# A graph-attention layer on one core: the tail of its first part re-ordered, W loaded in eight pieces

## The chip, the cores and the metric

The kernel runs on one core of a Trainium2 chip. A core has five engines with a queue of their own each: TensorE (PE in the profile, its weight loads PEld), VectorE (DVE), ScalarE (ACT), GpSimd (POOL) and SyncE (SP, which here only issues DMAs). An engine executes its queue in order; between engines there are semaphores. The metric is the device time of the whole kernel in microseconds; lower is better.

## The reference

There are N = 3327 nodes with D = 1024 features. adj is an N x N int32 matrix of zeros and ones with some 17 ones in a row. All else is float32.

```python
h = jnp.maximum(_layernorm(x, axis=-1), 0.0)
f = h @ Wf + bf
g = h @ Wg + bg
e = jax.nn.relu(f @ g.T)
scores = jnp.where(adj > 0, e, NEG)
attention = jax.nn.softmax(scores, axis=1)
out = x + attention @ (h @ W + bW)
```

## The kernel before

Only the neighbours of a node count, so the kernel (`edge_path`) turns each row of adj into a list of neighbours, and then gathers the rows of h that a list names. It has two parts, and each engine's order of work is written out by hand in both.

**Part 1** goes through the rows in NT = 26 tiles of 128 nodes (the last has 127) in stages i = 0 to 22. For each tile:

- `load_adj` brings 128 x 3327 integers into one of five buffers (`kpool`, tiles named r). It is issued by SP five stages ahead, when the buffer's former tile has been searched.
- `degrees` (ScalarE, L691) turns the integers to floats and counts them; `keys` (GpSimd, L698) multiplies the row by 1 to N, in two halves.
- `segments` (VectorE, L761) takes the eight largest keys out of each of 16 stretches of a row; `listed` (VectorE, L768 to L776) makes a list of 24 out of these 128 and writes it to pay. `store_lists` and `store_left` (SP) write the lists to pd and the candidates to cd, both in DRAM.
- layernorm: `load_x` (SP, six buffers in `ln`, tiles named xt); `measured` and `rooted` compute mean and deviation, on VectorE for odd tiles (L707, L709) and in two passes on ScalarE for even ones (L721 to L725); `inverted` (VectorE, L729) takes the reciprocal; `scaled` (ScalarE, L735) writes h in place; `store_h` (SP, L739) stores it to hd in DRAM.

The tables `at_load`, `at_stats` and `at_scale` say in which stage a tile's x is loaded, measured and scaled. Beside this, TensorE multiplies Wf by the transposed Wg in stages 4 to 21 (`product`, L831; the result is A_sb, and WgT is the tile that W_sb takes over).

**The order of the nodes.** Nodes are sorted by degree. `one_hot` (L784) makes a row of 48 bins from a degree; `before` and `after` (TensorE, L792 and L795) count with it into pre; `placed` (L800) takes a node's place among those of its own degree. The tail of part 1 (from L965) does this for the last tiles, then sums over bins (L1015 to L1022), makes rank, lo and hi (L1024 to L1028), compares them with a counting row (ohp at L1034, ohs and place at L1040 to L1046), and 26 small multiplications (L1049) invert the order into perm (L1057). In the tail stand also the searches of tiles 23, 24 (`late`) and 25 (`last`) and the layernorm of the last tiles.

**Part 2** takes 26 tiles of 128 nodes in the order of perm. For each tile it gathers lists from pd (ps), candidates from cd for nodes of high degree (cts), and rows of hd (G) with indirect DMAs that GpSimd issues (L635), one per list place. q = h A + b is TensorE's (L1209); scores are dot products on VectorE (L1222); ScalarE takes the exponential and weighs rows; TensorE sums and transposes them (L1260) and multiplies by W (L1287). The order comes from a planner (`planned`), and is the same before and after the change. The first two tiles' q are made ahead (L1069 to L1092) from two gathers of hd, which stand first in GpSimd's queue after perm; then, in the kernel before, comes the load of W as one DMA of 4 MB (L1064), then the first list gather. bWb, the broadcast bias of W, is loaded by SP (L1124).

SP's DMAs share eight semaphores in turn: each issue waits until the DMA eight before it has landed, and SP's queue is in order.

Of the kernel before, what the change touches and what calls it, by code (L numbers as in the profile page):

```python
# [575 lines left out]
def edge_path(ctx: ExitStack, tc: tile.TileContext, x, adj, Wf, bf, Wg, bg, W, bW, out, flag):  # L576
# [67 lines left out]
    with ExitStack() as part1:  # L644
# [33 lines left out]
        def load_x(t):  # L678
            xt = xs[t] = ln.tile([P, D], FP, name="xt")
            for b, m in pieces(t):  # L680
                nc.sync.dma_start(xt[b : b + m], x[t * P + b : t * P + b + m, :])
# [168 lines left out]
        at_load = {t: t + 2 for t in range(18)} | {18: 20, 19: 21, 20: 21, 21: 22, 22: 22, 23: 22, 24: 22}  # L850
        at_stats = {t: t + 4 for t in range(16)} | {16: 20, 17: 20, 18: 21, 19: 22, 20: 22}
        at_scale = {t: t + 5 for t in range(16)} | {16: 21, 17: 21, 18: 22}
        of = lambda table, i: [t for t in range(NT) if table.get(t) == i]

        with tc.manual_schedule(engines={
# [59 lines left out]
            for i in range(NT - 3):  # L915
                degrees(i + 2)
                keys(i + 2, nc.gpsimd)
                if i < 3:
                    for c in (2 * i + 2, 2 * i + 3):
                        transposed(WgT[:, :, c * P : (c + 1) * P], A_sb[:, c, :D])  # L920
                        empty()
# [15 lines left out]
                if i + 5 < NT:  # L937
                    load_adj(i + 5)
                for c in range(KD):
# [23 lines left out]
                for t in of(at_load, i):  # L963
                    load_x(t) if t >= NT - 3 else None
            late, last = NT - 2, NT - 1  # L965
            degrees(last)
            keys(last, nc.gpsimd)
            empty()
            one_hot(late, last)
            one_hot(last, NT)  # L970
            for t in (NT - 7, NT - 6):
                inverted(t)
                scaled(t)
            store_left(NT - 4)
            store_h(NT - 7)
            load_x(last)
            store_h(NT - 6)
            measured(NT - 5, True)
            rooted(NT - 5)
            measured(NT - 4, False)  # L980
            rooted(NT - 4)

            s = 0
            after(counted - 1)
            for t in range(counted, NT):
                before(t)
                segments(NT - 3, s, s + 2)
                s += 2
                placed(t)
                after(t)  # L990
                if t == NT - 3:
                    for u in (NT - 5, NT - 4):
                        inverted(u)
                    for u in (NT - 5, NT - 4):
                        scaled(u)
                        store_h(u)
            segments(NT - 3, s, s + 1)
            measured(NT - 3, True)
            rooted(NT - 3)
            measured(late, False)  # L1000
            rooted(late)

# [15 lines left out]
            inverted(NT - 3)  # L1018
            scaled(NT - 3)
            store_h(NT - 3)  # L1020
# [3 lines left out]
            nc.vector.tensor_add(ranki, rank, rp)  # L1024
            lo = c1.tile([P, NT], I32, name="lo")
            nc.vector.tensor_scalar(lo, ranki, P - 1, None, op0=ALU.bitwise_and)
            hi = c1.tile([P, NT], I32, name="hi")
            nc.vector.tensor_scalar(hi, ranki, 7, None, op0=ALU.logical_shift_right)  # L1028
            inverted(late)
            scaled(late)  # L1030
            store_h(late)
            measured(last, True)
            rooted(last)
            nc.vector.tensor_tensor(  # L1034
                ohp, lo[:, :, None].to_broadcast([P, NT, P]), iotap[:, None, :].to_broadcast([P, NT, P]), op=ALU.is_equal
            )
            inverted(last)
            scaled(last)
            store_h(last)
# [5 lines left out]
            )  # L1045
            nc.vector.tensor_scalar(place[:, :, 1, :], ohs, part, None, op0=ALU.mult)  # L1046
            ps = p_mm.tile([P, CB], FP, name="ps_A")
            for t in range(NT):
                nc.tensor.matmul(  # L1049
                    ps[:, : 2 * NT], ohp[:, t, :], place[:, t, :, :].rearrange("p a s -> p (a s)"),  # L1050
# [321 lines left out]
```

## Time and profile before

| | |
|---|---|
| median of 3 runs | 1243.84 us (1241.71 to 1244.11) |
| the profiled execution | 1279.55 us, span 1277.8 us, mean TensorE clock 0.951 |
| PE, DVE, ACT, POOL busy | 88%, 89%, 48%, 69% of the span |
| DMA | 374.46 MB, mean 293 GB/s |
| adj, x loads, h stores: median from issue to landing | 13.2, 13.5, 10.5 us |

The profile is of one execution, and its times count from the span's start. Part 1 lies from 0 to some 230 us; part 2 follows and overlaps with its end. A row of a timeline gives start and length, engine, line, operation, output and input, and in brackets how long the engine was idle before it and what ended this. A DMA's row is that of its issue; its data land later. The granted clock concerns TensorE alone.

### The profile page before, as it was taken

Reading aid. Unit: us, or ns where it says so; the run is one execution under the profiler, and the core shown is the slowest. Engines: PE = TensorE matmul, PEld = TensorE weight load, DVE = VectorE, ACT = ScalarE, POOL = GpSimd, SP = SyncE. Lnnn points to the kernel's source line nnn. Section 1 sums busy time; section 2 is a strip of 40 time slices with the busy share of each in tenths; the row PEclk is TensorE's granted clock in tenths of the full one; section 3 lists DMA queues with packets and bytes.
Section 4 is the critical chain, followed back from the end, with each engine's and each line's share of the span. In section 5 each row is a group of like instructions: output and inputs, shape, how many; then the busy total and the mean of one; then the engine's idle time right before and its main releaser. Section 6 shows DMA issues by size and latency. Waiting matters only on the chain. (4 is left out here: it accounts for less than half of the span.)

```text
span 1277.8 us, 14478 instructions
## 1 busy us (share of the span) xinstructions
PE 1127.0 (88%) x4632; PEld 720.7 (56%) x4632; DVE 1134.0 (89%) x2167; ACT 618.1 (48%) x941; POOL 876.2 (69%) x677
## 2 busy tenths in 40 slices
PE   2799980887987899997999799999999999999995
PEld 2566650555646467655766465665655665555553
DVE  6999977778798999999999979898999999999991
ACT  5899978234418256544644254453323433333250
POOL 8999975277576667677677657557676776766711
PEclk9899985798998999999999899999999999989998
DMA  9999996689768989989899879679987998989941
GB/s 369 418 379 397 404 347 233 209 313 340 268 204 298 340 274 328 313 311 311 284 325 293 305 221 332 216 259 330 311 299 236 339 270 305 271 291 296 321 110 52
DMA packets 101803, 374.46 MB, mean 293 GB/s; under 512 B 14747, under 2 KB 18490, under 8 KB 98519
## 3 DMA queue, kind: packets, MB, share of 16 engines
q0 software_dynamic: 80624, 290.96, 67.9%
q1 hardware_dynamic: 21094, 82.49, 17.1%
q8 instruction: 38, 0.62, 0.2%
q14 instruction: 47, 0.39, 0.1%
HBM read 344.11 MB, written 29.30 MB: 292 GB/s over the span
## 5 line engine op out<-in xcount | busy, mean ns | idle before, releaser
L635 POOL DMA_INDIRECT G<-hd,ps x454 | 524.3, 1155 | 243.6 <-issue 103.1
L1222 DVE CUSTOM_DVE_ANT_0 junk<-G,q 128x1024 bf16<-128x1024 f32 x468 | 601.6, 1286 | 40.0 <-DMA G<-hd,ps 28.7
L1209 PE MATMUL p_q<-A_sb,hT 128*128 128x342 f32 x1152 | 361.1, 463 | 14.7 <-ACT hT L1205 5.2
L1287 PE MATMUL p_o<-W_sb,yT 128*128 128x512 f32 x832 | 368.2, 598 | 3.7 <-ACT yT L1283 3.3
L1272 DVE SCALAR_TENSOR_TENSOR G<-G,sc 128x1024 f32<-128x1024 f32 x257 | 330.9, 1287 | 11.5 <-ACT G L1245 10.4
L1209 PEld LDWEIGHTS p_q<-A_sb,hT 128*128 128x128 f32 x1152 | 217.5, 195 | 124.0 <-issue 17.4
L1287 PEld LDWEIGHTS p_o<-W_sb,yT 128*128 128x128 f32 x832 | 158.2, 192 | 194.3 <-issue 184.7
L1260 PE MATMUL p_y<-ident,G 128*128 128x128 f32 x1688 | 208.2, 276 | 21.4 <-issue 11.5
L1260 PEld LDWEIGHTS p_y<-ident,G 128*128 128x128 f32 x1688 | 192.5, 143 | 53.5 <-issue 25.5
L1256 ACT ACTIVATE G<-G,sc 128x1024 f32<-128x1024 f32 x185 | 197.2, 1137 | 0.1
L698 POOL TENSOR_TENSOR r<-r,iotaj 128x1664 f32<-128x1664 f32 (+3 forms) x50 | 183.8, 3762 | 15.0 <-ACT r L691 15.0
L1298 ACT ACTIVATE xp<-p_o,rs 128x512 f32<-128x512 f32 x50 | 33.1, 682 | 213.1 <-DMA out_dram<-xp,perm 80.9
L831 PE MATMUL ps_A<-WgT,WfT 128*128 128x342 f32 x432 | 132.2, 465 | 2.4 <-ACT WfT L826 2.4
L761 DVE MAX8 cand<-r 128x8 f32<-128x208 f32 (+2 forms) x416 | 119.1, 360 | 4.0 <-POOL r L698 3.7
L831 PEld LDWEIGHTS ps_A<-WgT,WfT 128*128 128x128 f32 x432 | 82.5, 195 | 43.5 <-issue 3.3
L1215 ACT COPY q<-p_q 128x342 f32<-128x342 f32 x72 | 31.8, 445 | 128.0 <-PE p_q L1209 51.5
L691 ACT ACTIVATE r<-r 128x3327 f32<-128x3327 int32 (+3 forms) x27 | 77.3, 2862 | 8.1 <-DMA r<-in_adj_dram 8.1
L1283 ACT COPY yT<-p_y 128x512 f32<-128x512 f32 x52 | 29.9, 585 | 75.6 <-remote 43.9
L1205 ACT COPY hT<-p_t 128x512 f32<-128x512 f32 x48 | 27.4, 587 | 67.7 <-PE p_q L1209 32.4
L635 POOL DMA_INDIRECT xp<-in_x_dram,perm x25 | 41.5, 1660 | 22.1 <-ACT xp L1298 15.0
L1202 PE MATMUL p_t<-ident,G 128*128 128x128 f32 x192 | 31.7, 289 | 24.6 <-ACT hT L1205 9.1
L1305 POOL DMA_INDIRECT out_dram<-xp,perm x25 | 31.0, 1239 | 30.3 <-DMA xp<-in_x_dram,perm 22.9
(139 smaller groups left out, 687.2 us busy)
## 6 DMA issues: line engine op xcount, KB each, us to landing
r<-in_adj_dram SPq DMA_DIRECT2D x24, 1663.5 KB, 13.2
xt<-in_x_dram SPq DMA_DIRECT2D x25, 512.0 KB, 13.5
hd<-xt SPq DMA_DIRECT2D x25, 512.0 KB, 10.5
G<-hd,ps POOLq DMA_INDIRECT x454
A_sb<-in_L_gnn_Wg_dram SPq DMA_DIRECT2D x8, 512.0 KB, 17.4
A_sb<-in_L_gnn_Wf_dram SPq DMA_DIRECT2D x8, 512.0 KB, 12.1
W_sb<-in_L_gnn_W_dram POOLq DMA_DIRECT2D x1, 4096.0 KB
cd<-cand SPq DMA_DIRECT2D x25, 64.0 KB, 12.5
```

Of the source, the lines that this page charges most:

```text
L635: return nc.gpsimd.indirect_dma_start(out=to, out_offset=None, in_=table, in_offset=bass.IndirectOffsetOnAxis(ap=idx, axis=0), **kw,)
L691: nc.scalar.activation(r[:n, b:e], a[:n, b:e], AF.Sign, accum_out=to)
L698: eng.tensor_mul(r[:n, b:e], r[:n, b:e], iotaj[:n, b:e])
L761: nc.vector.max(cands[t][:n, s * 8 : s * 8 + 8], r[:n, s * SW : min(N, (s + 1) * SW)])
L831: nc.tensor.matmul(ps[:, :QB], WfTs[c][:, k, :], WgT[:, k, o : o + QB], start=(k == 0), stop=(k == KD - 1))
L1209: nc.tensor.matmul(ps_q[(3 * t + i) % 2][:, :QB], hT[:, k, :], A_sb[:, k, i * QB : (i + 1) * QB], start=False, stop=(k == KD - 1), skip_gr ...
L1222: nc.vector.tensor_tensor_reduce(junk, row(t, k), q[:, :D], 1.0, q[:, D : D + 1], op0=ALU.mult, op1=ALU.add, accum_out=scs[t % 3][:, k : k ...
L1256: nc.scalar.activation(g, g, AF.Copy, scale=scs[t % 3][:, k : k + 1])
L1260: nc.tensor.matmul(ps_y[g][:, c, :], of[:, (4 * g + c) * P : (4 * g + c + 1) * P], ident, is_transpose=True, start=((t, g) not in begun an ...
L1272: nc.vector.scalar_tensor_tensor(y, row(t, k), scs[t % 3][:, k : k + 1], y, op0=ALU.mult, op1=ALU.add)
L1287: nc.tensor.matmul(ps_o[o], yT[:, k, :], W_sb[:, k, o * CB : (o + 1) * CB], start=False, stop=(k == KD - 1), skip_group_check=True,)
L1298: nc.scalar.activation(to, ps_o[o], AF.Copy, scale=rss[t % 3])
```

## The change

All of it lies in the order of part 1's end; the sums are the same.

- The tables change: tile 17 is measured in stage 21 and scaled in 22, tile 18 measured in 22; tiles 18 to 25 are scaled in the tail. x of 22 and 23 is loaded in stage 21.
- `degrees` and `keys` of the last tile come in stage 22, behind those of tile 24.
- After tile 21's searches its adj buffer becomes `spare`, and x of tiles 19, 20 and 21 goes there.
- W is loaded by SP in eight pieces of 512 KB, put between the last stores of h, where GpSimd issued one DMA behind the first two gathers.
- The four ranks of the tail stand among four searches each of tile 23 (they stood among two each, the other seven searches standing behind place). Layernorm of the last tiles is spread over the tail anew.
- The compare ohp is cut in three (10, 10 and 6 tiles), each with its multiplications behind it; the listing of tile 23 stands ahead of perm.

```diff
--- before.py
+++ after.py
@@ -676,7 +676,9 @@
                     nc.sync.dma_start(r.bitcast(I32)[b : b + m, c0:c1_], adj[t * P + b : t * P + b + m, c0:c1_])
 
         def load_x(t):
-            xt = xs[t] = ln.tile([P, D], FP, name="xt")
+            if t not in xs:
+                xs[t] = ln.tile([P, D], FP, name="xt")
+            xt = xs[t]
             for b, m in pieces(t):
                 nc.sync.dma_start(xt[b : b + m], x[t * P + b : t * P + b + m, :])
 
@@ -847,9 +849,9 @@
             plan[S0 + j * (S1 - S0) // len(steps)].append(step)
         wants = {c: i for i in plan for step in plan[i] if step[0] is factor for c in [step[1]]}
 
-        at_load = {t: t + 2 for t in range(18)} | {18: 20, 19: 21, 20: 21, 21: 22, 22: 22, 23: 22, 24: 22}
-        at_stats = {t: t + 4 for t in range(16)} | {16: 20, 17: 20, 18: 21, 19: 22, 20: 22}
-        at_scale = {t: t + 5 for t in range(16)} | {16: 21, 17: 21, 18: 22}
+        at_load = {t: t + 2 for t in range(18)} | {18: 20, 22: 21, 23: 21, 24: 22}
+        at_stats = {t: t + 4 for t in range(16)} | {16: 20, 17: 21, 18: 22}
+        at_scale = {t: t + 5 for t in range(16)} | {16: 21, 17: 22}
         of = lambda table, i: [t for t in range(NT) if table.get(t) == i]
 
         with tc.manual_schedule(engines={
@@ -915,6 +917,9 @@
             for i in range(NT - 3):
                 degrees(i + 2)
                 keys(i + 2, nc.gpsimd)
+                if i == NT - 4:
+                    degrees(NT - 1)
+                    keys(NT - 1, nc.gpsimd)
                 if i < 3:
                     for c in (2 * i + 2, 2 * i + 3):
                         transposed(WgT[:, :, c * P : (c + 1) * P], A_sb[:, c, :D])
@@ -936,6 +941,11 @@
                 segments(i, SEG // 2, SEG)
                 if i + 5 < NT:
                     load_adj(i + 5)
+                if i == NT - 5:
+                    spare = kpool.tile([P, N], FP, name="r")
+                    for u in range(NT - 7, NT - 4):
+                        xs[u] = spare[:, (u - NT + 7) * D : (u - NT + 8) * D]
+                        load_x(u)
                 for c in range(KD):
                     if wants[c] - 2 == i:
                         load_w(Wf, c)
@@ -962,44 +972,41 @@
                     store_h(t)
                 for t in of(at_load, i):
                     load_x(t) if t >= NT - 3 else None
+            W_sb = wgpool.tile([P, KD, QW], FP, tag="wg", name="W_sb")[:, :, :O]
+
+            def load_W(k):
+                nc.sync.dma_start(W_sb[:, k, :], W[k * P : (k + 1) * P, :])
+
             late, last = NT - 2, NT - 1
-            degrees(last)
-            keys(last, nc.gpsimd)
             empty()
+            load_x(last)
+            for k in range(2):
+                load_W(k)
             one_hot(late, last)
             one_hot(last, NT)
-            for t in (NT - 7, NT - 6):
-                inverted(t)
-                scaled(t)
-            store_left(NT - 4)
-            store_h(NT - 7)
-            load_x(last)
-            store_h(NT - 6)
-            measured(NT - 5, True)
-            rooted(NT - 5)
-            measured(NT - 4, False)
-            rooted(NT - 4)
-
+            measured(19, True)
+            rooted(19)
+            inverted(18)
             s = 0
             after(counted - 1)
             for t in range(counted, NT):
                 before(t)
-                segments(NT - 3, s, s + 2)
-                s += 2
+                segments(NT - 3, s, s + 4)
+                s += 4
                 placed(t)
                 after(t)
-                if t == NT - 3:
-                    for u in (NT - 5, NT - 4):
-                        inverted(u)
-                    for u in (NT - 5, NT - 4):
-                        scaled(u)
-                        store_h(u)
-            segments(NT - 3, s, s + 1)
-            measured(NT - 3, True)
-            rooted(NT - 3)
-            measured(late, False)
-            rooted(late)
-
+                if t == NT - 4:
+                    inverted(19)
+                    measured(21, True)
+            scaled(18)
+            store_left(NT - 4)
+            store_h(18)
+            scaled(19)
+            store_h(19)
+            load_W(2)
+            measured(20, False)
+            rooted(20)
+            rooted(21)
             work = kpool.tile([P, N], FP, name="r")
             above = work[:, : NT * NBIN].rearrange("p (t d) -> p t d", d=NBIN)
             wide = work.bitcast(BF)[:, 2 * NT * NBIN :]
@@ -1015,42 +1022,65 @@
             nc.vector.tensor_tensor_scan(incl, onesd, pre, 0.0, op0=ALU.mult, op1=ALU.add)
             nc.vector.tensor_scalar(incl, incl, -1.0, float(N), op0=ALU.mult, op1=ALU.add)
             nc.vector.tensor_mul(above, oh, incl[:, None, :].to_broadcast([P, NT, NBIN]))
-            inverted(NT - 3)
-            scaled(NT - 3)
-            store_h(NT - 3)
+            inverted(20)
+            scaled(20)
+            store_h(20)
+            inverted(21)
+            scaled(21)
+            store_h(21)
+            load_W(3)
+            measured(23, True)
             rank = c1.tile([P, NT], FP, name="rank")
             nc.vector.tensor_reduce(rank, above, AX.X, ALU.add)
             ranki = c1.tile([P, NT], I32, name="ranki")
             nc.vector.tensor_add(ranki, rank, rp)
+            hi = c1.tile([P, NT], I32, name="hi")
+            nc.vector.tensor_scalar(hi, ranki, 7, None, op0=ALU.logical_shift_right)
             lo = c1.tile([P, NT], I32, name="lo")
             nc.vector.tensor_scalar(lo, ranki, P - 1, None, op0=ALU.bitwise_and)
-            hi = c1.tile([P, NT], I32, name="hi")
-            nc.vector.tensor_scalar(hi, ranki, 7, None, op0=ALU.logical_shift_right)
-            inverted(late)
-            scaled(late)
-            store_h(late)
-            measured(last, True)
-            rooted(last)
-            nc.vector.tensor_tensor(
-                ohp, lo[:, :, None].to_broadcast([P, NT, P]), iotap[:, None, :].to_broadcast([P, NT, P]), op=ALU.is_equal
-            )
-            inverted(last)
-            scaled(last)
-            store_h(last)
+            measured(22, False)
+            rooted(22)
+            rooted(23)
             nc.vector.tensor_tensor(
                 ohs, hi[:, :, None].to_broadcast([P, NT, NT]), iotap[:, None, :NT].to_broadcast([P, NT, NT]), op=ALU.is_equal
             )
             nc.vector.tensor_tensor(
                 place[:, :, 0, :], ohs, iotap[:, :NT, None].to_broadcast([P, NT, NT]), op=ALU.mult
             )
+            inverted(22)
+            scaled(22)
+            store_h(22)
+            load_W(4)
+            inverted(23)
+            scaled(23)
+            store_h(23)
+            load_W(5)
             nc.vector.tensor_scalar(place[:, :, 1, :], ohs, part, None, op0=ALU.mult)
+            measured(last, True)
+            measured(late, False)
+            rooted(late)
+            rooted(last)
             ps = p_mm.tile([P, CB], FP, name="ps_A")
-            for t in range(NT):
-                nc.tensor.matmul(
-                    ps[:, : 2 * NT], ohp[:, t, :], place[:, t, :, :].rearrange("p a s -> p (a s)"),
-                    start=(t == 0), stop=(t == NT - 1),
-                )
-            segments(NT - 3, s + 1, SEG)
+            for t0, t1 in ((0, 10), (10, 20), (20, NT)):
+                nc.vector.tensor_tensor(
+                    ohp[:, t0:t1, :], lo[:, t0:t1, None].to_broadcast([P, t1 - t0, P]),
+                    iotap[:, None, :].to_broadcast([P, t1 - t0, P]), op=ALU.is_equal,
+                )
+                for t in range(t0, t1):
+                    nc.tensor.matmul(
+                        ps[:, : 2 * NT], ohp[:, t, :], place[:, t, :, :].rearrange("p a s -> p (a s)"),
+                        start=(t == 0), stop=(t == NT - 1),
+                    )
+                if t1 == 20:
+                    inverted(late)
+                    scaled(late)
+                    store_h(late)
+                    inverted(last)
+                    scaled(last)
+                    store_h(last)
+                    for k in range(6, KD):
+                        load_W(k)
+            listed(NT - 3)
             tens = c1.tile([P, NT], FP, name="tens")
             nc.vector.tensor_copy(tens, ps[:, NT : 2 * NT])
             nc.vector.scalar_tensor_tensor(tens, ps[:, :NT], float(P), tens, op0=ALU.mult, op1=ALU.add)
@@ -1060,8 +1090,6 @@
             for s in ORDER[:2]:
                 hps.append(ln.tile([P, D], FP, name="xt"))
                 gather(hps[-1], hd[:, :], perm[:, s : s + 1])
-            W_sb = wgpool.tile([P, KD, QW], FP, tag="wg", name="W_sb")[:, :, :O]
-            nc.gpsimd.dma_start(W_sb, W.rearrange("(k p) o -> p k o", p=P))
 
             def bank(i, fresh):
                 ps = p_mm.tile([P, CB], FP, name="ps_A")
@@ -1093,7 +1121,6 @@
                 if j < 2:
                     pq.append(bank(j + 1, False))
 
-            listed(NT - 3)
             store_lists(NT - 2 - BATCH, NT - 2)
             store_left(NT - 3)
             segments(late, 0, SEG)
```

## The prediction

> **What bounds the kernel now.** I read the share of busy time in 40 slices first, then the chain that ended last, then the windows and the engines' timelines around 150 to 300 us, where the edited lines run. The chain reaches back only to 1087.8 us and is matrix multiplications, so it says nothing on part 1. The windows of the whole core (length, busy time of PE, PEld, DVE, ACT, POOL, then clock, DMA share, GB/s) give the stages:
>
> ```profile
> 165.00:170.00 5.00, 5.00 (x21) 3.23 (x20) 4.64 (x19) 3.96 (x6) 5.00 (x2) 1.00 1.02 421
> 175.00:180.00 5.00, 3.74 (x14) 2.20 (x13) 0.00 (x0) 0.84 (x3) 3.93 (x2) 1.00 1.05 292
> 205.00:210.00 5.00, 0.48 (x4) 0.29 (x4) 3.08 (x15) 4.68 (x10) 5.00 (x2) 0.50 0.26 105
> 240.00:245.00 5.00, 5.00 (x21) 3.36 (x20) 4.62 (x23) 0.03 (x1) 0.00 (x0) 0.90 1.04 411
> 250.00:255.00 5.00, 5.00 (x19) 3.23 (x18) 0.52 (x2) 1.29 (x3) 3.67 (x4) 1.00 0.14 22
> ```
>
> Up to 175 us POOL (keys) and the DMA are both full. At 175 VectorE does nothing for a whole window. From 200 to 230 the DMA is half empty; at 240 W fills it; at 250 it is nearly idle, because part 2's gathers have not begun. The timelines name the waits (start, length, then in brackets the idle time and what ended it):
>
> ```profile
> 165.12 0.33 SPq L681 DMA_DIRECT2D xt<-in_x_dram  x1
> 180.98 1.29 DVE L707 BATCH_NORM_STATS2 st<-xt 128x6 f32<-128x512 f32 x2 [7.38 <-DMA xt<-in_x_dram]
> 185.97 7.37 POOL L698 TENSOR_TENSOR r<-r,iotaj 128x1664 f32<-128x1664 f32 x2 [7.04 <-ACT r L691]
> 204.88 0.21 DVE L784 TENSOR_TENSOR oh<-held,pay 127x48 bf16<-127x48 f32 x1 [3.46 <-ACT r L691]
> 211.40 0.16 DVE L729 RECIPROCAL rstd<-rstd 128x1 f32<-128x1 f32 x1 [2.71 <-ACT rstd L725]
> 227.76 0.18 DVE L1057 TENSOR_SCALAR perm<-tens 128x26 int32<-128x26 f32 x1
> 229.43 1.08 POOL L635 DMA_INDIRECT xt<-hd,perm  x1 [17.16 <-DVE held L772]
> 243.77 0.18 DVE L776 TENSOR_SCALAR pay<-held 127x24 int32<-127x24 f32 x1
> 250.42 1.01 POOL L635 DMA_INDIRECT ps<-pd,perm  x1 [17.67 <-DMA cd<-cand]
> 258.62 1.28 DVE L1222 CUSTOM_DVE_ANT_0 junk<-G,q 128x1024 bf16<-128x1024 f32 x1 [1.80 <-DMA G<-hd,ps]
> ```
>
> Two gates open part 2. The first gather of lists (250.42) waits for the last lists, which VectorE ends at 243.95, and their store, landing 5.2 us after issue beside W. The first gather of ordered rows (229.43) waits for perm (227.94) and the last h store, issued at 225.5 and landing 2.9 us later. After 250.42 POOL issues gathers every 1.3 us without a gap until 308, and VectorE waits for them 13.6 us between 190 and 320. So part 2's start hangs on the 250.42 gate. The multiplications of its first two tiles, from 235.0 to 268.4, hang on the other.
>
> **What the skill says.** In the Trainium skill, "DMA: Bandwidth & Descriptors", section "Queues, rings and completion order", descriptors of one ring are consumed in ring order. The trace agrees: x of tile 17, issued 0.7 us behind adj of tile 24, landed 15.8 us later, some 3 us behind that adj. Section "Where 436 GB/s comes from" gives 435 as the fabric's ceiling; the trace shows 421 at share 1.02. So I take this backlog as the kernel's, not the profiler's. Section "Anatomy of one DMA" gives some 2.0 us of fixed cost; the quickest transfer on h here, between 140 and 260 us, landed in 2.6 us. "VectorE: DVE Perf Modes", section on the TRN2 errata, gives each instruction a fixed latency; small ones take 0.14 to 0.2 us here, which prices the split compare.
>
> **The change, part by part**, in times of the profiled execution.
>
> *Statistics of x moved.* Tile 17's go from stage i=20 to 21. VectorE ended its searches of stage 20 at 173.6; now listing (2.1) and ranks (0.1) follow, then stage 21's searches (4.6) to 180.3, and the wait for x 17, landing near 180.95, shrinks from 7.38 to 0.7 us. ScalarE had the same hole (6.67) behind tile 17's mean, and POOL behind ScalarE (7.04); both close. Stage 21 ends at 184.8, not 192.2: -7.4. Stage 22 loses tile 19's statistics (1.5) too and ends near 192.9, not 201.4.
>
> *Last tile's degrees and keys in stage 22.* ScalarE does degrees of 24 and 25 back to back (3.1 each). Adj 25 landed at 187.75, where SP's queue passed it, and ScalarE would be there at 186.1: a new wait of 1.7 us, with the scaling of tile 17 and all later layernorm queued behind it. Degrees 25 end at 190.9, so the 3.46 wait of the one-hot at 204.88 goes: VectorE has it at 193.1, not 205.1. POOL's keys 25 end near 201, needed near 229.
>
> *Layernorm of tiles 18 to 25 all in the tail.* This takes part of the gain back. On ScalarE behind degrees 25: an accumulator eviction 0.4, then one scaling 1.5 (17), four two-pass statistics of 3.0 (18, 20, 22, 24), four short ones of 0.4, and six scalings of 1.5 (18 to 23), 24.5 us; waiting some 3 us for VectorE's reciprocals of 19 and 20, it reaches rstd of 25 near 218.3. VectorE, from 193.1: four statistics 6.0, 16 searches 4.6, four ranks 1.1, reciprocals 1.2, scan to small integers 3.9, shifted one-hots 2.1, compare 3.57 plus two extra instructions at 0.15, listing of tile 23 at 2.3, perm 0.55, together 25.6; and waits for ScalarE's rstd of 18, 22 and 24 of 1.4, 1.1 and 1.2. Perm stands at 222.4, not 227.94: -5.5. Tile 23's listing ahead of perm delays it 2.3 but covers the last six small multiplications (26 took 1.31); it is off the path to the lists, being only moved. Scaling of 24 and 25 ends near 221.4, not 225.1, so the last h store and the first gather of rows come 3.7 earlier.
>
> *Spare adj buffer.* x 19 to 21 get room when tile 21's searches end, 180.3. On SP they stand behind h 15, whose turn came at 181.0, so x 19 issues at 181.4 as now and lands near 192.4 if what is queued ahead (adj 25, x 18, h 15) moves at 400 GB/s. It is wanted at 193.1. Later x loads stop waiting for h stores (9.9 us of SP waits from 150 to 320). The buffers that work and compare take are one tile younger, searched by 203 and wanted from there: nothing.
>
> *W in eight pieces on SP.* 4 MB at 400 GB/s is 10.5 us of DMA, moved from 232-248 into the half-empty 200-230; the rest of POOL's queue loses one 0.96 us issue. Pieces stand among h stores: each may hold the store behind it 1.3 us, and each issue of SP waits for the eighth DMA before it. Ahead of the last two h stores stand W 2 to 5, spread over 203-216, so I cost this at nothing; if none had drained, 5.3 us on the row gate. W 6 and 7 and the stores of lists come behind. The bias load moves behind the last list store, some 242, where it takes 1.3 us of DMA from the first gathers.
>
> *The sum.* Lists: perm at 222.4 plus two tiles' searches and listings, 13.7 as now (243.95 less 227.94 less 2.3), give 236.1, not 243.95: -7.9. Their store no longer lands beside W: 5.2 becomes between 2.6 and 5.2; I take 3.5, so the gate opens 9.6 early. Less 1.3 for the bias load: -8.3. The row gate opens 3.7 early, so the first q stands near 251.4 and the second near 265.2; VectorE's first dot moves 7.2, the later ones follow their rows, and TensorE, which had some 12 us of idle time between 268 and 310, gives up part of it. I take -7.6 for the end. The profiled execution's span goes from 1277.8 (1279.55 with what lies around it) to some 1270. It is 36 us above the median of 1243.84, a difference I can't place; the gain is one shift of the start, so I carry it over whole: 1243.84 - 7.6 = 1236.2.
>
> **Rivals.** (a) The 7.38 stall is the profiler's: in a plain run x 17 lands in time, the tail before starts 7.4 earlier and only the rest is gained. Then lists come 0.5 and W's removal 1.7 earlier, some 2.5 with ScalarE's shorter wait for adj, rows 1.5 later: -1 to -4, 1241.3. For it: the 36 us. Against: DMA at its ceiling from 20 to 175 us, and x landing in a median of 13.5 us against a stage of 7.5. (b) TensorE takes the pace: rows come only 3.7 early, and if its 12 us idle time is really work missing from the records, -3.7: 1240.1. Against: ScalarE and POOL idle there too. (c) Slower: x 19 lands late. VectorE's statistics of 19 stand ahead of all tile 23's searches, ranks and lists. x 19 has 0.7 us, then 1.4 that the wait for rstd 18 absorbs, then 8.3 of gain; landing after 203, 22 us behind its issue, the kernel loses. At 206 it costs 3: 1247. Against: the longest x landing was 15.8. (d) It doesn't do what it says: the gathers' start is hidden by later slack and nothing shows, 1243.8. Against: POOL's gapless issue up to 308.
>
> **Numbers.** Forecast 0.61, (a) 0.17, (b) 0.09, (c) 0.07, (d) 0.06. The forecast's own range is -5 to -11 (landing of the list store 2.6 to 5.2, ScalarE's waits twice or none): 1233 to 1239. With (a) and (b) the range is 1232 to 1242.5. About 0.2%, 2.5 us, is what a measurement of this kernel can tell from no change. Faster by more: the forecast, most of (b), some 0.6 of (a): 0.80. Within: the rest of (a), (d): 0.13. Slower: (c): 0.07.
>
> **What would show it.** No VectorE wait above 2 us for x near 175; one-hot of tile 25 near 193; perm near 222; first row gather near 226, first list gather near 241; W's eight pieces landed before 230; then POOL's gathers gapless. The prediction is wrong if x 19 or an rstd holds VectorE longer, if an h store sits behind W, or if an early list gather meets TensorE or q late, so that idle time grows between 250 and 310.

## The result, and the profile after

The changed kernel takes 1232.36 us, the median of four runs (1231.06 to 1234.84), against 1243.53 for the kernel before (1241.71 to 1244.11). The ratio is 0.991, with a 95% interval of 0.989 to 0.9931: 11.2 us less, 8.6 to 13.7. The forecast was 7.6 less. A run more than 1.5% above the fastest of its kernel counts as slow, and the ratios here and below leave such runs out. The profiled execution took 1231.06 us, its span 1229.3. That of before took 1279.55, so the spans of the two pages can't be set against each other. The times up to 230 us can, and those of the start of part 2: what lengthens the profiled execution of before comes later, as told below.

The same five windows as before the change, in the profile after (length, busy time of PE, PEld, DVE, ACT, POOL, clock, DMA share, GB/s):

```profile
165.00:170.00 5.00, 5.00 (x20) 3.25 (x19) 4.76 (x21) 4.08 (x7) 5.00 (x2) 1.00 1.02 420
175.00:180.00 5.00, 5.00 (x21) 3.23 (x20) 4.52 (x19) 4.97 (x7) 5.00 (x3) 1.00 1.05 268
205.00:210.00 5.00, 0.00 (x0) 0.00 (x0) 4.47 (x9) 4.90 (x8) 0.00 (x0) 0.50 1.03 419
240.00:245.00 5.00, 5.00 (x24) 3.57 (x23) 2.00 (x10) 1.87 (x4) 3.78 (x5) 1.00 0.53 122
250.00:255.00 5.00, 5.00 (x19) 3.32 (x18) 3.12 (x5) 0.44 (x1) 4.09 (x4) 1.00 1.03 414
```

VectorE's empty window at 175 is gone. At 205 the DMA is full (0.26 before): W's pieces are among what moves there. At 250 the gathers of part 2 run at 414 GB/s, where there was next to nothing (22). The timelines' rows that answer to those of before, and at the end the 21st and the 25th dot product:

```profile
180.88 6.80 SPq L683 DMA_DIRECT2D r<-in_x_dram  x3
180.41 1.29 DVE L709 BATCH_NORM_STATS2 st<-xt 128x6 f32<-128x512 f32 x2 [0.89 <-DMA xt<-in_x_dram]
149.58 51.40 POOL L700 TENSOR_TENSOR r<-r,iotaj 128x1664 f32<-128x1664 f32 x14
192.12 0.32 DVE L786 TENSOR_TENSOR oh<-held,pay 128x48 bf16<-128x48 f32 x2
195.69 0.16 DVE L731 RECIPROCAL rstd<-rstd 128x1 f32<-128x1 f32 x1 [1.37 <-ACT rstd L727]
220.66 0.18 DVE L1087 TENSOR_SCALAR perm<-tens 128x26 int32<-128x26 f32 x1
225.50 1.07 POOL L635 DMA_INDIRECT xt<-hd,perm  x1 [24.53 <-DVE cand L763]
234.31 0.18 DVE L778 TENSOR_SCALAR pay<-held 127x24 int32<-127x24 f32 x1
237.26 0.99 POOL L635 DMA_INDIRECT ps<-pd,perm  x1 [9.42 <-DMA cd<-cand]
251.81 1.28 DVE L1249 CUSTOM_DVE_ANT_0 junk<-G,q 128x1024 bf16<-128x1024 f32 x1 [8.51 <-ACT q L1120]
265.25 0.15 DVE L1346 CAST flag<-p_y 1x1 int32<-1x1 f32 x1 [5.50 <-PE p_y L1182]
287.55 1.30 DVE L1249 CUSTOM_DVE_ANT_0 junk<-G,q 128x1024 bf16<-128x1024 f32 x1 [1.62 <-ACT q L1242]
292.88 1.28 DVE L1249 CUSTOM_DVE_ANT_0 junk<-G,q 128x1024 bf16<-128x1024 f32 x1
```

x of tiles 19 to 21 goes into the spare buffer from 180.88 on. The wait for x of tile 17 is 0.89 us and no longer 7.38; GpSimd has its keys without a hole up to 201; perm ends at 220.84 and not 227.94. The row gate (the first gather of ordered rows) opens at 225.50 (before 229.43), the list gate (the first gather of lists) at 237.26 (before 250.42). What VectorE waits for at the start of part 2 is another thing now: before it was rows of the lists (G), now it is TensorE's work, first q (8.51 us), then the product for the flag (5.50), then q of the third tile (1.62). From 250 to 310 us TensorE is busy for 58.45 of the 60 us, against 49.61 before.

In the kernel before, these waits go on for 40 us (the same view of before, four of ten rows, and the 25th dot product):

```profile
262.17 1.28 DVE L1222 CUSTOM_DVE_ANT_0 junk<-G,q 128x1024 bf16<-128x1024 f32 x1 [2.25 <-DMA G<-hd,ps]
269.32 1.28 DVE L1222 CUSTOM_DVE_ANT_0 junk<-G,q 128x1024 bf16<-128x1024 f32 x1 [1.67 <-DMA G<-hd,ps]
282.28 1.29 DVE L1222 CUSTOM_DVE_ANT_0 junk<-G,q 128x1024 bf16<-128x1024 f32 x1 [1.18 <-DMA G<-hd,ps]
296.46 1.28 DVE L1222 CUSTOM_DVE_ANT_0 junk<-G,q 128x1024 bf16<-128x1024 f32 x1 [4.54 <-DMA G<-hd,ps]
304.53 1.28 DVE L1222 CUSTOM_DVE_ANT_0 junk<-G,q 128x1024 bf16<-128x1024 f32 x1
```

After the change VectorE has no wait on G up to the 25th dot product, which begins at 292.88: 11.6 us sooner than 304.53. From there to the end of the span it is 936.4 us. If the kernel before needs the same from 304.5, its span is 1240.9 and its time, with the 1.75 around it, 1242.7; 1243.53 was measured. So the whole gain seems to be there by the 25th dot product. That the rest takes as long in both kernels is an assumption: there is no profile of the kernel before from a chip like that of the result.

### The profile page after: what moved, and what is told of

It is laid out like the page before. It is cut to its first block, busy times and chain, and to the rows that moved or that the text cites. A ratio compares the mean times of both kernels' runs of the same rounds, so it can differ in the third digit from the quotient of the medians.

```text
span 1229.3 us, 14490 instructions
## 1 busy us (share of the span) xinstructions
PE 1110.1 (90%) x4632; PEld 711.3 (58%) x4632; DVE 1132.5 (92%) x2169; ACT 617.6 (50%) x941; POOL 872.2 (71%) x676
## 5 line engine op out<-in xcount | busy, mean ns | idle before, releaser
L1236 PE MATMUL p_q<-A_sb,hT 128*128 128x342 f32 x1152 | 351.8, 454 | 3.1 <-ACT p_q L1245 2.5
L1236 PEld LDWEIGHTS p_q<-A_sb,hT 128*128 128x128 f32 x1152 | 213.4, 191 | 107.1 <-issue 9.1
L833 PE MATMUL ps_A<-WgT,WfT 128*128 128x342 f32 x432 | 129.5, 458 | 2.4 <-ACT WfT L828 2.4
L1268 ACT ACTIVATE sc<-sc,nm 128x10 f32<-128x10 f32 (+10 forms) x36 | 11.0, 306 | 111.6 <-DVE nm L1258 98.0
## 6 DMA issues: line engine op xcount, KB each, us to landing
A_sb<-in_L_gnn_Wf_dram SPq DMA_DIRECT2D x8, 512.0 KB, 11.6
```

The lines of the kernel that those rows point to most:

```text
L833: nc.tensor.matmul(ps[:, :QB], WfTs[c][:, k, :], WgT[:, k, o : o + QB], start=(k == 0), stop=(k == KD - 1))
L1236: nc.tensor.matmul(ps_q[(3 * t + i) % 2][:, :QB], hT[:, k, :], A_sb[:, k, i * QB : (i + 1) * QB], start=False, stop=(k == KD - 1), skip_gr ...
```

## The experiments

Eight of the runs were on two chips on which the kernel before takes 1268 us (1256 to 1289) and the changed one 1264. The other four, with the degrees in the tail, the slowed gathers, the list of tile 23 and the second run of the flag, were on two chips like that of the result (1242). The 25 us come with stops of TensorE and ScalarE in part 2, told of below. So times are compared as ratios to the kernel before on the same chip, and the traces, where no early stop disturbs them, across chips. The expectations for after_again, a_rowlate and a_listlate speak of the 49th dot product; I had miscounted, their numbers are those of the 25th.

**The kernel before again**, unchanged.

> The kernel before, unchanged, for a second profile. Theory: the 36 us between its first profiled execution and its median belong to that one execution's part 2; this span is 1239 to 1245, with the wait for x of tile 17 again near 7 us, the first row gather near 229 and the first list gather near 250. Rival: profiling costs this kernel some 36 us always, or the wait for x 17 comes and goes with the execution; the span is near 1278, or that wait is below 2 us.

Measured: span 1263.0; the wait for x 17 was 6.45 us, perm ended at 226.14, row gate 227.62, list gate 248.59. The stall comes again and both gates come 1.8 us earlier, so they are not of one execution alone. A second profile can't tell whether the profiler makes the stall, which is rival (a). The result speaks against it: rival (a) allowed a gain of 1 to 4 us, and 8.6 to 13.7 were measured. The span of 1239 to 1245 did not come on this chip.

**Before, with the statistics of tile 17 moved alone.**

```diff
-        at_stats = {...} | {16: 20, 17: 20, 18: 21, 19: 22, 20: 22}
-        at_scale = {...} | {16: 21, 17: 21, 18: 22}
+        at_stats = {...} | {16: 20, 17: 21, 18: 21, 19: 22, 20: 22}
+        at_scale = {...} | {16: 21, 17: 22, 18: 22}
```

> The kernel before with tile 17 measured in stage 21 and scaled in 22, nothing else. Theory: the 7.4 us hole of stage 20 is in every execution, and behind it both gates move together: 5 to 7.4 us below before, 1236 to 1238.5. Rival (a), the hole is the profiler's: within 1 us of before.

Measured: 1271.02 us, ratio 1.0027 (1.0 to 1.0055): no gain, where 5 to 7.4 us were expected. The time alone would fit rival (a) too; the rows of VectorE and GpSimd give another reason:

```profile
179.88 1.29 DVE L707 BATCH_NORM_STATS2 st<-xt 128x6 f32<-128x512 f32 x2 [0.45 <-DMA xt<-in_x_dram]
192.07 0.16 DVE L729 RECIPROCAL rstd<-rstd 128x1 f32<-128x1 f32 x1 [5.45 <-ACT rstd L725]
195.08 7.34 POOL L698 TENSOR_TENSOR r<-r,iotaj 128x1664 f32<-128x1664 f32 x2 [8.76 <-ACT r L691]
204.40 0.21 DVE L784 TENSOR_TENSOR oh<-held,pay 127x48 bf16<-127x48 f32 x1 [5.71 <-ACT r L691]
```

The hole at x 17 is gone, and one of 5.45 us stands a stage later, behind ScalarE's statistics of tile 18, whose x is late next; GpSimd's hole moves with it. Perm ends at 227.46, between the two runs of before (227.94, 226.14).

**After, with the statistics of tile 17 put back** to stage 20.

```diff
-        at_stats = {t: t + 4 for t in range(16)} | {16: 20, 17: 21, 18: 22}
+        at_stats = {t: t + 4 for t in range(16)} | {16: 20, 17: 20, 18: 22}
```

> The changed kernel with tile 17 measured in stage 20 again. Theory: the hole comes back at 7 us in stage 20, but some 2.6 us of it are taken by ScalarE's wait for adj 25, which then goes: 4 to 5 us above the changed kernel, 1236.5 to 1237.5. Rival (a): within 1 us of it, 1232.

Measured: 1269.09 us, ratio 1.0019 (0.9989 to 1.0049), where the changed kernel has 0.9973 (0.995 to 0.9997; its run is below). The wait for x 17 is back:

```profile
178.32 1.28 DVE L709 BATCH_NORM_STATS2 st<-xt 128x6 f32<-128x512 f32 x2 [5.48 <-DMA xt<-in_x_dram]
196.80 0.32 DVE L786 TENSOR_TENSOR oh<-held,pay 128x48 bf16<-128x48 f32 x2
223.38 0.18 DVE L1087 TENSOR_SCALAR perm<-tens 128x26 int32<-128x26 f32 x1
```

The one-hot of tile 25 is 4.7 us later than in the changed kernel, perm, which ends at 223.56, some 2 later than the mean of the seven runs with the changed order up to perm (221.4, from 219.6 to 223.2). How much of this becomes time is not shown, since an early stop fell into this run. So the move made alone gains nothing and hands the hole on to x 18; among the other edits it gains some 2 us at perm.

**After, with the degrees and keys of the last tile behind the loop.**

```diff
-                if i == NT - 4:
-                    degrees(NT - 1)
-                    keys(NT - 1, nc.gpsimd)
...
+            degrees(last)
+            keys(last, nc.gpsimd)
             empty()
```

> The changed kernel with the last tile's degrees and keys behind the loop again, as before. My prediction's step 'last tile's degrees and keys in stage 22' makes the one-hot of tile 25 wait for them: one-hot at 200 to 205 instead of 192, a wait of 3 to 8 us on VectorE; perm 3 to 6 us later (224 to 226), row and list gate both later by as much, time 3 to 6 us longer than the changed kernel's 1264 here. Rival 'the keys' place is nothing, since what VectorE has of other work covers them': perm within 1 us of 220, time within 2.

Measured: 1233.0 us, ratio 0.9925 (0.9913 to 0.9937), beside 0.991 (0.989 to 0.9931) for the changed kernel.

```profile
194.51 0.21 DVE L786 TENSOR_TENSOR oh<-held,pay 127x48 bf16<-127x48 f32 x1 [3.52 <-ACT r L693]
220.98 0.18 DVE L1086 TENSOR_SCALAR perm<-tens 128x26 int32<-128x26 f32 x1
237.59 0.99 POOL L635 DMA_INDIRECT ps<-pd,perm  x1 [9.09 <-DMA cd<-cand]
```

The wait of 3.52 us is there, but the one of 1.37 behind it, for the reciprocal of tile 18, is gone in turn, and perm and both gates come 0.3 to 0.7 us later than in the changed kernel. The rival holds: taken back alone, this edit costs 0.3 us at perm, and the ratios, 0.15% apart, don't tell the two kernels apart.

**The changed kernel again, and three kernels beside it.** In the first (a_rowlate), ScalarE copies the first tile of ordered rows onto itself eight times; in the second (a_listlate), fifteen key searches of the last tile are done three times; in the third (a_W_one), W is loaded as before. The changed kernel itself (after_again) stands first.

> The changed kernel as it is, the anchor for the three runs beside it. Every theory: row gate (first gather of ordered rows) near 225.5 us, list gate (first gather of lists) near 237.3, VectorE's first dot near 251.8 after a wait of some 8.5 for ScalarE's q, its 49th dot near 292.9; time 0.991 of the kernel before (0.987 to 0.995). If TensorE and ScalarE again stand for ten or more us between 250 and 285 with no cause in the profile, the first dots come that much later and the time is up to 2% longer, as in the two runs of its variants so far.

Measured: 1264.05 us (1252.4 to 1270.44), ratio 0.9973 (0.995 to 0.9997). Row gate 224.41, list gate 236.06; then TensorE stopped inside the second q, and the 25th dot product came at 303.2.

```diff
             pq = [bank(i, True) for i in range(3)]
+            for _ in range(8):
+                nc.scalar.copy(hps[0], hps[0])
             transposed(hTs[0], hps[0])
```

> The changed kernel with the first tile of ordered rows copied onto itself eight times by ScalarE before TensorE transposes it: some 8 us (eight copies of 128x1024 at about 1.0) on the path from the row gate to q, nothing on the lists. Theory 'two gates, equal after the change' (the 49th dot comes at the later of row gate + 67.4 and list gate + 54.4, which the changed kernel has at 292.9 and 291.7): 49th dot near 301, time 7 to 8 us longer than the changed kernel beside it. Rival 'gathers of lists set the pace, q waits for nothing that counts': under 2 us longer. Rival 'q alone sets the start' (the sum of my prediction): 8 us longer as well.

Measured: 1271.22 us, ratio 1.0028 (1.0004 to 1.0053): 0.55% or 7 us above the changed kernel. The eight copies took 8.58 us. But they moved the other gate too:

```profile
244.08 0.96 POOL L635 DMA_INDIRECT ps<-pd,perm  x1 [15.35 <-ACT WfT L818]
```

The list gather waits for ScalarE's copies of that tile's transposes, which I had not seen: the gate opened at 244.08, 8.65 us behind the last list and not 2.77. So this run delays rows and lists together and can't tell q from lists; an early stop fell into it too.

```diff
             segments(last, 0, SEG)
+            for _ in range(2):
+                segments(last, 1, SEG)
             listed(last)
```

> The changed kernel with fifteen of the sixteen key searches of the last tile done three times instead of once: 30 more searches of 0.28 us, 8.4 us on the list gate (237.3 to 245.7), nothing on the rows. Theory 'two gates, equal after the change': 49th dot at list gate + 54.4 = 300.1 instead of 292.9, time 7 us longer than the changed kernel beside it. Rival 'q alone sets the start' (the sum of my prediction): first lists' rows land some 8 us after the list gate, 254 against q at 251.8, and the second q at 265 is untouched, so 0 to 2.5 us longer. Rival 'gathers of lists alone': 8.4 longer.

Measured: list gate 247.42 with the row gate at 227.12. The ratio, 0.9971 (0.9938 to 1.0004), is from 13 of 22 runs and equals that of the changed kernel; the median over all 22 is 1270.68, 6.6 above it. The two disagree, so the time settles nothing. The trace does: there was no early stop in it, and VectorE waits for rows of lists again as in the kernel before, the 25th dot product coming at 301.9, 54.5 behind the list gate.

```profile
255.80 1.28 DVE L1251 CUSTOM_DVE_ANT_0 junk<-G,q 128x1024 bf16<-128x1024 f32 x1 [1.75 <-DMA G<-hd,ps]
259.30 1.28 DVE L1251 CUSTOM_DVE_ANT_0 junk<-G,q 128x1024 bf16<-128x1024 f32 x1 [2.20 <-DMA G<-hd,ps]
293.85 1.28 DVE L1251 CUSTOM_DVE_ANT_0 junk<-G,q 128x1024 bf16<-128x1024 f32 x1 [5.02 <-DMA G<-hd,ps]
```

```diff
-            for k in range(2):
-                load_W(k)
...
                 gather(hps[-1], hd[:, :], perm[:, s : s + 1])
+            nc.gpsimd.dma_start(W_sb, W.rearrange("(k p) o -> p k o", p=P))
```

> The changed kernel with W loaded as before, in one transfer that GpSimd issues behind the two row gathers. Theory 'the eight pieces give the lists their early gate': the store of the last lists lands beside 4 MB of W again, 5 us after its issue instead of 1.4, so the list gate moves from 237.3 to 240 to 242, and by list gate + 54.4 the time is 2 to 5 us longer than the changed kernel beside it; the h stores before the row gate land sooner, so the row gate moves to 222.5 to 225. Rival 'W moved is free either way' (what my prediction took): within 1.5 us, list gate within 1 us.

Measured: 1265.93 us, ratio 0.9951 (0.9923 to 0.9978), so no difference in time from the changed kernel on this chip that the intervals show. With a stop in this trace as well, what the eight pieces are worth in time stays open. The gates moved both ways:

```profile
225.23 1.08 POOL L635 DMA_INDIRECT xt<-hd,perm  x1 [24.50 <-DMA cd<-cand]
227.58 0.96 POOL L1085 DMA_DIRECT2D W_sb<-in_L_gnn_W_dram  x1
242.67 1.00 POOL L635 DMA_INDIRECT ps<-pd,perm  x1 [14.14 <-DMA pd<-pay]
```

With W in one piece the list gate opens 7.22 us behind the last list (2.77 in the changed kernel and in all its other variants but a_rowlate): the eight pieces bring it forward by 4.45. In return the row gate opens 4.0 us behind the issue of the last h store (221.25) and not 5.2 (220.29 to 225.50 in the changed kernel), and TensorE has the first row tile 4.6 behind the gate and not 6.2: together 2.8 us that q starts later with the pieces, which are still landing then. The changed kernel on the same chip as this run has nearly the same two distances, 5.3 and 6.1.

**Gathers of the first two lists slowed**, by a memset on GpSimd behind each.

```diff
         def fetch(t, k):
             gather(row(t, k), hd[:, :], entry(t, k))
+            if t < 2:
+                nc.gpsimd.memset(idle, 0.0)
```

> The changed kernel with a GpSimd memset of 128x256 (some 0.4 us) behind each of the gathers of the first two lists, so that 28 gathers of 512 KB are issued every 1.65 us or so and not every 1.25, 315 GB/s and not 415. Theory 'saturation': on this chip TensorE and ScalarE stand from 258 to 275 because the gathers, with nothing taking rows until q is there, hold the DMA engines at a share of 1.02 for 15 us or more; paced, the share stays under 1, ScalarE copies q every 4.6 us without a stop, first dot near 251, second q near 264, 25th dot at 291 to 295 and not 303, time 6 to 10 us under the changed kernel's 1264 here. Rival 'the stops belong to this chip whatever the gathers do': first dots as late as before, time within 2 us of 1264 or up to 3 longer. Rival 'gathers are the pace': no stop, but rows late by up to 11 us, time 3 to 8 longer.

Measured: 1232.76 us, ratio 0.9938 (0.9918 to 0.9959), on a chip where the stops don't come, so that the question it was made for stays open. The memset cost less than thought: a gather every 1.44 us instead of 1.25. The 25th dot product came at 293.0, as in the changed kernel (292.9). After the change the gathers have that much room; they are not the pace.

**List of tile 23 taken behind perm.**

```diff
-            listed(NT - 3)
             tens = c1.tile([P, NT], FP, name="tens")
...
+            listed(NT - 3)
             segments(late, 0, SEG)
```

> The changed kernel with the list of tile 23 taken behind perm and not ahead of it: 2.3 us of VectorE's work moved from before the row gate to behind it. Theory 'two gates, equal after the change': perm and row gate 2.3 us earlier (218.4 and 223), list gate as it was, so the 25th dot is held by the list gate and gains 1 us at most; time within 2 us of the changed kernel's 1264 here. Rival 'q alone sets the start' (the sum of my prediction): 2.3 us shorter.

Measured: 1231.14 us, ratio 0.9906 (0.9892 to 0.992): the same as the changed kernel. Perm ended at 220.05, but the row gate opened at 226.35, 6.3 behind it: that is 5.1 behind the issue of the last store of h (221.22), as in the changed kernel (5.2). So by these times the row gate waits for that store and not for perm, and neither forecast of this run was put to the test, since the gate did not move forward.

**VectorE's copy of the flag moved** behind the first list's maximum, run twice.

```diff
+        told_at = next(i for i, step in enumerate(plan) if step[1][0] == "fl")
+        step = plan.pop(told_at)
+        first_sum = next(i for i, other in enumerate(plan) if other[1][0] == "S")
...
+        plan.insert(first_sum + 1, step)
```

> The changed kernel with VectorE's copy of the flag put behind the first tile's maximum instead of between its sixth and seventh dot product. Theory: since lists now come 13 us earlier but rows only 4, TensorE's q is what part 2 starts on, and VectorE waits 5.5 us at this copy with six dots ready behind it; taking the wait away gains 2 to 5 us, 1227.5 to 1230.5. Rival: TensorE, 90% busy, paces part 2 whatever VectorE does there: within 1 us of the changed kernel, 1232.

Measured: 1263.5 us, ratio 0.9941 (0.9909 to 0.9973); an early stop put the first dot product at 269.2, so nothing is told.

> The changed kernel with VectorE's copy of the flag moved behind the first list's maximum, once more, since the stop of TensorE and ScalarE hid its effect the first time. In the changed kernel VectorE stands 5.50 us at 259.74 for that copy, with six more rows of the first list behind it, and the 25th dot came at 292.9 with no stop. Theory 'VectorE sets the pace from the first q on': the six rows are taken meanwhile, dots 7 to 12 end near 268 and not 273, 25th dot near 288 to 290 if the gathered rows are there, time 3 to 5.5 us under the changed kernel's 0.991 of before, so 0.987 to 0.989. Rival 'rows of the lists set the pace' (list gate + 54.4 = 291.7): 25th dot at 291 to 292, 0 to 1.5 us under, 0.990 to 0.991. If the stop comes again, the first dot is near 269 and the ratio says nothing on either.

Measured: 1231.49 us, ratio 0.9909 (0.9889 to 0.9928): the same as the changed kernel.

```profile
270.04 0.13 DVE L1346 CAST flag<-p_y 1x1 int32<-1x1 f32 x1
272.73 0.16 DVE L1279 RECIPROCAL rs<-l 128x1 f32<-128x1 f32 x1 [2.56 <-ACT sc L1268]
288.92 1.28 DVE L1249 CUSTOM_DVE_ANT_0 junk<-G,q 128x1024 bf16<-128x1024 f32 x1 [4.46 <-ACT q L1242]
```

The 5.50 us in front of the flag are gone, and in their place VectorE waits 2.56 us for ScalarE and 4.46 for the third tile's q: what VectorE did sooner, it waits for later. Of the variants none is faster than the changed kernel by more than the intervals.

## What set the time, and the prediction's steps

The nine executions without an early stop fall in two groups (us; last q is the end of ScalarE's sixth copy of q):

| kernel | row gate | list gate | last q | 25th dot | behind last q | behind list gate |
|---|---|---|---|---|---|---|
| before | 229.4 | 250.4 | 268.9 | 304.5 | 35.7 | 54.1 |
| before again | 227.6 | 248.6 | 266.6 | 303.4 | 36.8 | 54.8 |
| before, tile 17 moved | 229.0 | 250.0 | 267.9 | 304.4 | 36.5 | 54.4 |
| after, lists late | 227.1 | 247.4 | 267.4 | 301.9 | 34.5 | 54.5 |
| after | 225.5 | 237.3 | 265.6 | 292.9 | 27.3 | 55.6 |
| after, degrees in the tail | 226.2 | 237.6 | 264.6 | 291.9 | 27.3 | 54.3 |
| after, list 23 late | 226.4 | 238.8 | 266.6 | 293.9 | 27.3 | 55.1 |
| after, gathers slowed | 225.4 | 237.1 | 265.6 | 293.0 | 27.4 | 55.9 |
| after, flag moved | 228.1 | 239.6 | 267.5 | 294.2 | 26.7 | 54.6 |

In the first four the 25th dot product stands 54.1 to 54.8 behind the list gate, with VectorE waiting for G; in the other five 26.7 to 27.4 behind the last q, whatever is done to flag, gathers or perm, with VectorE waiting for q. TensorE is busy for 49.6 to 53.9 us of the 60 from 250 to 310 in the first four and for 57.0 to 58.9 in the others. The fourth row is the experiment on this: it is the changed kernel with only the lists late, and it falls into the group of the kernel before. No run delays q alone, so that q sets the start after the change rests on these waits and the table.

The groups are also two kinds of chips: the first has those of the slower kind (the first row probably, see below), where every other run of the changed order met an early stop, and the second those of the faster kind. The gathers speak against the chip as the reason. The 19th gather of rows is issued 32.0 to 32.3 us behind the list gate in the first group and 27.3 to 28.6 in the second (the slowed run apart), but also 27.5 to 28.0 in four of the five stopped runs on the slower chips (30.3 in the one with W in one piece). And the slowed run brings the first group's pace (32.4) to a faster chip: there VectorE waits 1.29 us for G at the 19th dot product, then still 0.36 for q at the 21st, and the 25th stands where q puts it.

So before, lists set the start: with q alone it would have been, by estimate, 268.9 + 27.3 = 296.2. The change brought the lists forward until q took over (8.3 us) and q itself by 3.3 in these two executions: 11.6.

**Right.** Two gates open part 2, and before the change the list gate set its start; the kernel became faster. The measured 1232.36 us lies 0.6 us below the forecast's own range (1233 to 1239) and only 0.4 inside the wider one (1232 to 1242.5). Perm 5.5 earlier: 7.1 in the two profiles, but 5.6 between the mean of two runs of before (227.0) and of seven of the changed order (221.4). First q at 251.4 and second at 265.2: VectorE had them at 251.8 and, behind the flag, 265.3. The waits for rstd of 1.4, 1.1 and 1.2: 1.37, 0.93 and 1.20. *Spare adj buffer*: x 19 cost VectorE 0.35 us; rival (c) did not come.

**Wrong in size: *The sum*,** its term "I take 3.5" for the landing of the last lists' store. It landed in 1.4 to 1.6 us, below both of my ends (2.6 to 5.2): from last list to list gate 6.47 us became 2.77, so 3.7 were gained and not 1.7. The rest of the list gate's 13.2 against my 9.6 is perm, 1.6 earlier than worked out, which is inside the spread of executions (219.6 to 223.2). Put the measured gate into the sum in place of mine, and lists no longer bind; TensorE does, rival (b)'s engine, but at -11.6 and not at -3.7, because the row gate was far from binding before. This is one of the prediction's own signs of being wrong: the early list gather met q late, VectorE waited 8.51 us for it, and GpSimd's gathers, without a gap up to 308 us before, waited 12.2 us for TensorE and ScalarE between 250 and 310. So what ends the gain is not in the sum: the last wait ahead of the 25th dot product is for q. The idle time of TensorE between 268 and 310, "some 12 us" in the prediction, is 10.4 in the windows.

**Wrong in attribution: *Statistics of x moved*, "-7.4",** and ***Last tile's degrees and keys in stage 22*, "the 3.46 wait goes".** Both waits went, but not the time counted for them. The first edit is worth nothing alone and some 2 us at perm among the others; the second, taken back, costs 0.3 us at perm. What is late next stands right behind: x 18, then the degrees of 25. So most of the gain in perm is not the first edit's or the second's taken singly. Which of the remaining edits (layernorm spread anew, ranks among four searches, the compare in three) carries it was not separated.

**Wrong: *W in eight pieces*, "I cost this at nothing" for the row gate.** The last h store was issued 5.2 us earlier (225.52 to 220.29), not 3.7, but the gate follows it by 5.2 and not by 3.9 as in the kernel before. So the row gate gained 3.9, near the 3.7 forecast, by two errors that cancel, which is luck. The rows then land later too; with the pieces q starts 2.8 us later in all than in the run with W in one piece.

**The 36 us that I could not place** are most likely the chip's. The page of before has this line in its groups of instructions (busy, mean ns, idle before):

```profile
L1283 ACT COPY yT<-p_y 128x512 f32<-128x512 f32 x52 | 29.9, 585 | 75.6 <-remote 43.9
```

43.9 us of ScalarE's waits at this one copy ended with an event that no instruction of the trace made ("remote"); over all copies it is 91.2 us. The eight profiles from the two slower chips have 53 to 89 us of such waits of ScalarE; that of the result and the four from the faster chips have none. And 1279.55 us lies among the times of the kernel before on the slower chips, 1256 to 1289. So the profile of before was probably taken on a chip of that kind, though the record does not name it. The gain was not scaled by the 36 us, which was right.

## What to carry to other kernels

Before a stall is priced, look at who stands behind it: here several loads were late in a row, and moving one consumer alone handed the wait to the next and gained nothing. Where two chains open the next part, put both into one sum as a maximum, with the slack of each; the gain of the later one ends where the other begins. When a small store gates something, look at what else is in flight as it lands: here it took 1.4 to 1.6 us without W and 5.1 to 5.2 beside it, though the two stood in different queues. The megabytes then cost whoever shares their new place, here the last stores of h.

## What was not expected of the hardware

The last lists' stores (10.9 and 1.5 KB) landed in 1.6 and 1.4 us with the DMA nearly idle (share 0.11), and in 5.2 beside W. The Trainium skill's "DMA: Bandwidth & Descriptors", section "Anatomy of one DMA", gives some 2.0 us of fixed cost for a DMA that GpSimd issues; these stores are SP's, and for them the measurement decides.

TensorE can stop with nothing in the profile that it waits for. In the changed kernel on the slower chips (engine timeline of TensorE, then windows):

```profile
258.65 0.54 PE L1103 MATMUL ps_A<-A_sb,WfT 128*128 128x342 f32 x1 [0.29 <-issue]
261.42 0.73 PE L1103 MATMUL ps_A<-A_sb,WfT 128*128 128x342 f32 x1 [2.24 <-issue]
264.23 0.73 PE L1103 MATMUL ps_A<-A_sb,WfT 128*128 128x342 f32 x1 [2.07 <-issue]
...
269.82 5.60 PE L1103 MATMUL ps_A<-A_sb,WfT 128*128 128x342 f32 x10 [0.67 <-issue]
```

```profile
250.00:255.00 5.00, 5.00 (x19) 3.25 (x18) 0.00 (x0) 0.00 (x0) 3.78 (x5) 1.00 1.02 414
...
260.00:265.00 5.00, 1.46 (x2) 0.54 (x3) 4.15 (x8) 0.00 (x0) 4.03 (x4) 0.64 1.01 387
265.00:270.00 5.00, 1.63 (x3) 0.97 (x4) 0.00 (x0) 0.08 (x1) 1.01 (x2) 0.50 0.94 365
270.00:275.00 5.00, 5.00 (x10) 2.80 (x9) 0.00 (x0) 0.71 (x2) 0.00 (x0) 0.50 0.05 18
```

In one and the same chain a multiplication starts only every 1.4 to 2.8 us for 11 us, while the DMA share stands at 0.94 to 1.03. All 96 multiplications of the chain are in the trace, so none is merely missing from it. The granted clock falls to 0.5 meanwhile, and each then takes 0.73 us. All five kernels whose list gate opened before 245 us had a stop between 250 and 290 on these chips; the three with a later gate had none there, the changed kernel with late lists among them. That speaks for the gathers' load as a condition. But on the other chips the same load makes none (the kernel with list 23 late):

```profile
255.00:260.00 5.00, 5.00 (x19) 3.32 (x18) 4.86 (x9) 0.45 (x1) 3.88 (x4) 1.00 1.02 410
260.00:265.00 5.00, 5.00 (x19) 3.28 (x18) 0.73 (x2) 0.44 (x1) 3.78 (x5) 1.00 1.03 408
```

So the load is not enough, and the cause stays open. On the one of those two chips where the changed kernel itself ran, the change gains 0.27% (0.03 to 0.5) where it gains 0.9% elsewhere. There a stop took the earlier start away again: the 25th dot product came at 303.2 us, and at 303.4 in the kernel before on the other of the two.
